# A two-layer graph block: layer 0 and the output projection as seven half-size products, factors of q, k, v fetched per step, last norm moved off VectorE

## The chip, the cores and the metric

The kernel runs on one core of one Trainium2 chip. The time is the device time of one execution in microseconds (us); each kernel was run several times, and medians are quoted. The "span" of a profile is about 1.8 us shorter than the run that it was taken from, because it begins and ends at instructions.

Engine names in the profile: PE is TensorE's matmuls, PEld its weight loads, DVE is VectorE, ACT is ScalarE, POOL is GpSimd, SP is the engine whose queue issues the transfers ("the sync queue").

## The reference, cut to what matters

All values are float32: 128 batches of 128 nodes with 512 features, two layers, each added to its own input.

```python
# layer 0: mix over neighbours, then a 512 x 512 weight
h = maximum(layernorm(x), 0)
x = x + (einsum('nm,bmd->bnd', adj, h) @ weight + bias)
# layer 1: attention over the graph's edges, 8 heads of 64
h = maximum(layernorm(x), 0)
q, k, v = split(h @ w_qkv)                 # w_qkv is 512 x 1536
attn = softmax(where(adj == 0, -inf, q @ k.T * 64**-0.5))
o = (attn @ v) @ w_proj + b_proj           # w_proj is 512 x 512
x = x + o + layernorm(o) * ln_gamma + ln_beta
```

## The kernel before

Each batch passes through a long chain: norm, mix with the adjacency, layer 0, norm, an exchange through DRAM that turns rows into columns, q, k, v, scores, softmax, a second exchange, attention, projection, last norm. A plan with a time for each piece (one batch per "slot") fixes the program order on every engine, so that TensorE always has the work of some batch to do while the others wait.

q, k and v are made for a group of four batches by seven products of half-size blocks instead of eight (a Strassen form): sums of blocks of the left operand are made by GpSimd, the sums of the weights once at the start, and the results are put together by additions that read PSUM. Layer 0 and the projection are whole products of 512 columns:

```python
def product(g, kind, k, p):                 # one of the seven, for q, k, v
    left = LEFT[g][k]
    for half in range(2):
        for c in range(2):
            ...                             # lhsT or rhs from wqk_sb / wv_sb, resident in SBUF
            nc.tensor.matmul(p[:, half, :], lhsT=lhsT, rhs=rhs, ...)      # 256 columns

def layer0(i, t):
    p = mm_psum("pl0")
    for c in range(C):                      # C = 4 blocks of 128
        nc.tensor.matmul(p, lhsT=YT[i][:, c, :], rhs=w0_sb[:, c, :], start=(c == 0), stop=(c == C - 1))
    put(t + 3.7, norm1, i, t + 3.7, p)

def project(i, t):
    ...                                     # the same with OT[i] and wp_sb
    put(t + 3.7, finish, i, t + 3.7, p)

def finish(i, t, p):
    o = work.tile([P, D], F32, name="o")
    nc.vector.tensor_tensor(o, p, bp_b, op=ALU.add)
    mean, rs = stats_of(o)
    t_ = work.tile([P, D], F32, name="t", bufs=2)
    nc.vector.scalar_tensor_tensor(t_, o, mean, gamma_b, op0=ALU.subtract, op1=ALU.mult)
    nc.gpsimd.tensor_tensor(o, o, X1.pop(i), op=ALU.add)
    put(t + 8, finish_out, i, t_, rs, o)    # second scalar_tensor_tensor, then the store
...
SLOT = 19.0
for i in range(-LOAD, B + 3):
    t = i * SLOT
    at(t + 0.5, scores, i)
    at(t + 3, project, i - 2)
    at(t + 11, layer0, i + 8)
    at(t + 15.8, attend, i - 1)
    ...                                     # put(time, function, ...) sorts all pieces by time
```

## Time and profile before

| | before |
|---|---|
| time, median of 3 | 2561.32 us |
| span of the profile | 2558.2 us |
| busy: TensorE, VectorE, GpSimd, ScalarE | 98, 66, 45, 38% |
| matmul instructions | 12545 |
| work in TensorE's stream (see below) | 2475.3 us |
| lost while filling, in mid-run, while draining | 47.9, 0.0, 35.1 us |

The lines of the profile that carry this are shown in the prediction. Between two matmuls of the same shape that follow each other without a wait, the trace gives a start-to-start time: 429 ns for 512 columns, 216 for 256, 112 for 128. Add these over the whole program order, with the measured 1.09 us of a batch's scores and 1.03 of its attention and about 0.1 us for each switch into and out of these two (they use part of the array; the first of them starts 0.31 us after its full-size predecessor instead of 0.22, and after them the second full-size one 0.32 us after the first), and you have the time of the stream if TensorE never had to wait: its **work**. At any point of the program, the time in the trace less the work up to there is what has been **lost** so far, be it to waits or to a slow clock. Filling is what is lost before the scores of batch 8, mid-run from there to the scores of batch 124, draining the rest.

The seven-product form puts its weights' sums in SBUF beside the weights, and the transfers took less than half of the DMA engines' time. This line of the profile's page of before gives the queue's packets, its MB, and the share of the time of 16 engines:

```profile
q1 hardware_dynamic: 262288, 342.54, 41.3%
```

### The profile page before, as it was taken

The numbers are of one execution on the slowest core, as the hardware profiler recorded it, in microseconds if no ns is written. First come the engines' busy times: TensorE is split into PE (matmuls) and PEld (weight loads), VectorE is DVE, ScalarE is ACT, GpSimd is POOL, SyncE is SP. The second block draws the span as 40 slices with busy tenths as digits, with TensorE's granted clock in tenths as the row PEclk, the third lists the DMA queues.
The fourth block names the chain that finished last, engine by engine and source line by source line (L and its number), as shares of the span: only waits on it lengthen the run. The fifth ranks groups of instructions, "written<-read, shape, count | busy, mean of one in ns | idle before, by whom it ended". The sixth has DMA issues, their size and how long they took to land.

```text
span 2558.2 us, 36517 instructions
## 1 busy us (share of the span) xinstructions
PE 2497.8 (98%) x12545; PEld 1749.4 (68%) x12545; DVE 1676.1 (66%) x3119; ACT 962.3 (38%) x2946; POOL 1153.4 (45%) x1030
## 2 busy tenths in 40 slices
PE   5999999999999999999999999999999999999996
PEld 3677776766767767777677676676767667767673
DVE  4466666666666667666666666666666666666665
ACT  2243343343334343334334334333333433433331
POOL 3444444444445435444444444444544444444332
PEclk8999999999999999999999999999999999999997
DMA  5244444444443443444444444444344344444333
GB/s 187 93 137 141 145 127 132 148 133 132 144 137 124 145 144 124 139 143 130 137 145 131 132 141 139 132 141 140 124 136 148 128 135 146 132 132 137 123 100 106
DMA packets 262472, 344.86 MB, mean 135 GB/s; under 512 B 28944, under 2 KB 161168, under 8 KB 262288
## 3 DMA queue, kind: packets, MB, share of 16 engines
q1 hardware_dynamic: 262288, 342.54, 41.3%
q8 instruction: 99, 1.62, 0.3%
q14 instruction: 85, 0.70, 0.1%
HBM read 174.65 MB, written 167.77 MB: 134 GB/s over the span
## 4 chain that ended last, share of the span: by engine, by line
PE 94%; issue 2%; POOL 1%; DVE 1%; DMA 0%; SPq 0%; ACT 0%; POOLq 0%; DVEq 0%; ACTq 0%
PE cx L239 26%; PE pl L183 17%; PE pp L331 17%; PE cy L239 13%; PE cz L239 7%; PE ps L278 5%; PE po L322 5%; PE pmix L174 4%; POOL rs L143 0%; POOL e L307 0%; DMA h1x<-d 0%; POOL o L341 0%; SPq L155 0%; DVE st L137 0%; ACT h L161 0%
## 5 line engine op out<-in xcount | busy, mean ns | idle before, releaser
L143 POOL TENSOR_TENSOR rs<-ve,minus_half 128x1 f32<-128x1 f32 x384 | 261.7, 681 | 726.7 <-DVE ve L141 725.6
L183 PE MATMUL pl<-w_sb,yT 128*128 128x512 f32 x1024 | 465.5, 598 | 4.3 <-DVE x L189 4.3
L331 PE MATMUL pp<-wp_sb,oT 128*128 128x512 f32 x1024 | 466.9, 599 | 1.4 <-ACT oT L404 1.4
L298 ACT ACTIVATE e<-s,mx 128x128 f32<-128x128 f32 x1024 | 394.1, 386 | 29.2 <-DVE mx L289 24.7
L169 POOL TENSOR_TENSOR x<-x,b_b 128x512 f32<-128x512 f32 x128 | 162.3, 1268 | 465.9 <-ACT h L161 463.4
L161 ACT ACTIVATE h<-x,shift,rs 128x512 f32<-128x512 f32 x256 | 208.3, 814 | 416.0 <-DVE shift L160 400.5
L183 PEld LDWEIGHTS pl<-w_sb,yT 128*128 128x128 f32 x1024 | 196.2, 192 | 198.0 <-issue 186.8
L331 PEld LDWEIGHTS pp<-wp_sb,oT 128*128 128x128 f32 x1024 | 196.5, 192 | 196.1 <-issue 187.5
L286 DVE TENSOR_TENSOR s<-ps,maskb 128x512 f32<-128x512 f32 x256 | 164.5, 684 | 171.1 <-PE ps L278 171.1
L337 DVE TENSOR_TENSOR o<-pp,bp_b 128x512 f32<-128x512 f32 x128 | 88.5, 692 | 273.0 <-PE pp L331 273.0
L198 POOL TENSOR_TENSOR x<-x,beta_b 128x512 f32<-128x512 f32 x128 | 162.4, 1269 | 196.1 <-ACT h L161 196.1
L239 PE MATMUL cy<-sum,wqk_sb 128*128 128x256 f32 x1024 | 246.7, 384 | 3.9 <-POOL sum L221 3.9
L239 PE MATMUL cx<-sum,wqk_sb 128*128 128x256 f32 x1024 | 248.5, 385 | 1.8 <-ACT qkT L404 1.8
L404 ACT COPY qkT<-cx 128x512 f32<-128x512 f32 x192 | 111.8, 582 | 360.4 <-PE cx L239 360.4
L307 POOL TENSOR_TENSOR e<-e,sm 128x1024 f32<-128x1024 f32 x128 | 244.5, 1910 | 4.1 <-DVE sm L306 4.1
L239 PE MATMUL cx<-h1T,wqk_sb 128*128 128x256 f32 x1024 | 245.0, 382 | 0.0
L239 PEld LDWEIGHTS cy<-sum,wqk_sb 128*128 128x128 f32 x1024 | 193.0, 191 | 72.5 <-issue 44.0
L404 ACT COPY oT<-po 128x512 f32<-128x512 f32 x128 | 75.1, 587 | 438.9 <-PE po L322 438.9
L345 DVE SCALAR_TENSOR_TENSOR t<-t,rs,o 128x512 f32<-128x512 f32 x128 | 226.5, 1770 | 4.3 <-POOL o L341 4.3
L239 PEld LDWEIGHTS cx<-h1T,wqk_sb 128*128 128x128 f32 x1024 | 189.6, 190 | 54.0 <-issue 29.9
L239 PEld LDWEIGHTS cx<-sum,wqk_sb 128*128 128x128 f32 x1024 | 187.1, 190 | 47.4 <-issue 22.1
L298 ACT ACTIVATION_READ_ACCUMULATOR e<-s,mx 128x1 f32 x1024 | 191.1, 187 | 0.0
(68 smaller groups left out, 3596.3 us busy)
## 6 DMA issues: line engine op xcount, KB each, us to landing
d<-e SPq DMA_DIRECT2D x128, 512.0 KB, 2.6
sx<-d SPq DMA_DIRECT2D x512, 128.0 KB, 2.9
x<-in_x_dram SPq DMA_DIRECT2D x130, 256.0 KB, 2.9
d<-h SPq DMA_DIRECT2D x128, 256.0 KB, 2.3
x1d<-x SPq DMA_DIRECT2D x128, 256.0 KB, 2.0
h1x<-d SPq DMA_DIRECT2D x512, 64.0 KB, 2.4
x1b<-x1d SPq DMA_DIRECT2D x128, 256.0 KB, 2.8
out_dram<-t SPq DMA_DIRECT2D x128, 256.0 KB, 3.0
```

The costliest lines, as they stand in the source:

```text
L143: nc.gpsimd.tensor_tensor(rs, ve, minus_half, op=ALU.pow)
L161: nc.scalar.activation(dst, src, AF.Relu, bias=shift, scale=rs)
L169: put(t + 5, lambda: nc.gpsimd.tensor_tensor(x_, x_, b0_b, op=ALU.add))
L183: nc.tensor.matmul(p, lhsT=YT[i][:, c, :], rhs=w0_sb[:, c, :], start=(c == 0), stop=(c == C - 1))
L198: nc.gpsimd.tensor_tensor(X1[i], X1[i], beta_b, op=ALU.add)
L239: nc.tensor.matmul(p[:, half, :], lhsT=lhsT, rhs=rhs, start=first and half == 0 and c == 0, stop=k in (3, 5, 6) and c == 1, skip_group_che ...
L286: nc.vector.tensor_tensor(s[:, e * C:(e + 1) * C, :], ps[e], m4, op=ALU.add)
L298: nc.scalar.activation(e[:, :, h, :], s[:, h, :].rearrange("p (q r) -> p q r", q=Q), AF.Exp, bias=shift[:, h:h + 1], scale=scale, accum_ou ...
L307: nc.gpsimd.tensor_tensor(e, e, sm.unsqueeze(1).unsqueeze(3).to_broadcast([P, Q, H, R]), op=ALU.mult)
L331: nc.tensor.matmul(p, lhsT=OT[i][:, c, :], rhs=wp_sb[:, c, :], start=(c == 0), stop=(c == C - 1))
L345: nc.vector.scalar_tensor_tensor(t_, t_, rs, o, op0=ALU.mult, op1=ALU.add)
L404: f(*a)
```

## The change

Layer 0 and the projection now also go by seven half-size products, on pairs of batches. That needs room: seven blocks of factors for each of the two weights are resident, and in exchange the factors of q, k, v are no longer. Their four sums are made at the start and written to DRAM, and each of the 21 steps of a group fetches its own factor (256 KB), four steps ahead. The last norm leaves VectorE, which has the new additions to do: ScalarE normalizes, GpSimd multiplies by gamma and adds. The schedule is remade, with a compressed beginning (`FILL`) and an end of its own for the last four batches.

The core of the diff, cut (`...`):

```diff
-    wqk_sb = const.tile([P, 7, 2, D], F32)
-    wv_sb = const.tile([P, 7, 2, D // 2], F32)
-    wp_sb = const.tile([P, C, D], F32)
+    w0_sb = const.tile([P, 7, 2, F], F32)          # F = 256
+    wp_sb = const.tile([P, 7, 2, F], F32)
...
+    def fetch(g, kind, k):
+        t = WQ[g, kind, k] = work.tile([P, 2, F], F32, name="wq", bufs=5)
+        plain = {0: (0, 0), 3: (1, 1), 5: (1, 0)}
+        nc.sync.dma_start(out=t, in_=qkv_block(kind, *plain[k]) if k in plain else SUMS[kind, k])
...
+    def pair_left(j, t, src, left, name):          # four sums on GpSimd, 256 columns each
+        y = src.pop(j)
+        left[j] = left_factors(t, 1.7, y[:, 0:2, 0, :], y[:, 2:4, 0, :], y[:, 0:2, 1, :], y[:, 2:4, 1, :], name)
+
+    def pair_chain(left, w_sb, tiles, addend):
+        def product(k, p, first, last):
+            for c in range(2):
+                nc.tensor.matmul(p[:, 0, :], lhsT=left[k][:, c, :], rhs=w_sb[:, k, c, :], ...)
+        ...                                        # results by additions of 256 columns on VectorE
+        return seven({"x": "d0", "y": "d1", "z": "z"}, product, start, results, 1.0)
...
-        t_ = work.tile([P, D], F32, name="t", bufs=2)
-        nc.vector.scalar_tensor_tensor(t_, o, mean, gamma_b, op0=ALU.subtract, op1=ALU.mult)
-        nc.gpsimd.tensor_tensor(o, o, X1.pop(i), op=ALU.add)
-    def finish_out(i, t_, rs, o):
-        nc.vector.scalar_tensor_tensor(t_, t_, rs, o, op0=ALU.mult, op1=ALU.add)
+        put(t + 1, lambda: nc.gpsimd.tensor_tensor(x1, x1, o, op=ALU.add))
+    def finish_out(i, t, mean, rs, x1):
+        n = work.tile([P, D], F32, name="t", bufs=2)
+        norm(AF.Identity, n, O.pop(i), mean, rs)
+        put(t + 1.5, lambda: nc.gpsimd.tensor_tensor(n, n, gamma_b, op=ALU.mult))
+        put(t + 4, finish_last, i, n, x1)          # gpsimd: n + x1, then the store
...
-    SLOT = 19.0
+    SLOT, FILL = 18.2, 7.0
+    def scores_at(i):
+        return when(i, 0) if i < LAST else when(LAST, -0.05) + (i - LAST) * 8.5
...
+    for n, (t, *a) in enumerate(steps):
+        put(steps[n - 4][0] + 0.1 if n >= 4 else t - 10, fetch, *a)
+    for kind, t in enumerate((when(-9, 0.2), when(-4, 0.0), when(-2, 0.1))):
+        put(t, combine_qkv, t + 7, kind)
```

## The prediction

> **What bounds the kernel now.** I read the page first: the busy shares, the chain that ended last, and the costliest groups.
>
> ```profile
> span 2558.2 us, 36517 instructions
> PE 2497.8 (98%) x12545; PEld 1749.4 (68%) x12545; DVE 1676.1 (66%) x3119; ACT 962.3 (38%) x2946; POOL 1153.4 (45%) x1030
> PE 94%; issue 2%; POOL 1%; DVE 1%; DMA 0%; SPq 0%; ACT 0%; POOLq 0%; DVEq 0%; ACTq 0%
> L183 PE MATMUL pl<-w_sb,yT 128*128 128x512 f32 x1024 | 465.5, 598 | 4.3 <-DVE x L189 4.3
> L331 PE MATMUL pp<-wp_sb,oT 128*128 128x512 f32 x1024 | 466.9, 599 | 1.4 <-ACT oT L404 1.4
> L239 PE MATMUL cx<-sum,wqk_sb 128*128 128x256 f32 x1024 | 248.5, 385 | 1.8 <-ACT qkT L404 1.8
> ```
>
> TensorE fills the span and nearly the whole chain; VectorE, the next, is at 66%. So the time is what TensorE's stream costs plus the times it has no work. Layer 0 (L183) and project (L331) are the only whole products left; q, k, v (L239) already go by seven half-size products. Each fp32 matmul of the program is two instructions (1024 for 4 x 128).
>
> A group's mean (598 ns) is one instruction's latency, not its cost. The timeline of TensorE in mid-run gives the cost, from start to start:
>
> ```profile
> 1204.82 1.16 PE L278 MATMUL ps<-qkT 64*128 64x128 f32 x16
> 1205.91 1.99 PE L239 MATMUL cx<-h1T,wqk_sb 128*128 128x256 f32 x8
> 1207.74 3.60 PE L331 MATMUL pp<-wp_sb,oT 128*128 128x512 f32 x8
> 1211.17 1.89 PE L239 MATMUL cy<-sum,wqk_sb 128*128 128x256 f32 x8
> 1212.90 1.05 PE L174 MATMUL pmix<-adjT,h 128*128 128x128 f32 x8
> 1213.79 1.89 PE L239 MATMUL cx<-sum,wqk_sb 128*128 128x256 f32 x8
> 1215.52 3.60 PE L183 MATMUL pl<-w_sb,yT 128*128 128x512 f32 x8
> 1218.95 1.89 PE L239 MATMUL cy<-sum,wqk_sb 128*128 128x256 f32 x8
> ```
>
> No idle stands between them. A whole product takes 3.43 us (1211.17 - 1207.74; 429 ns per instruction of 512 columns), a q, k, v step 1.73 us (216 ns per 256), a mix 0.89. From pp to the next pp (1226.64) it is 18.90 us with five steps; a group of four batches has 21, so 0.25 x 1.73 more: 19.33 us per batch, x 128 = 2474 us.
>
> The rest, 2558 - 2474 = 84 us, is filling and draining. Windows show where:
>
> ```profile
> 0.00:60.00 60.00, 30.20 (x84) 17.08 (x85) 26.30 (x63) 11.54 (x17) 17.49 (x25) 0.87 0.55 189
> 60.00:120.00 60.00, 54.30 (x230) 40.18 (x229) 23.72 (x57) 19.16 (x42) 24.58 (x25) 0.96 0.27 88
> 2500.00:2530.00 30.00, 18.19 (x87) 10.67 (x87) 22.10 (x33) 10.73 (x50) 10.29 (x8) 0.82 0.35 117
> 2530.00:2558.00 28.00, 15.09 (x48) 6.89 (x47) 9.80 (x14) 1.17 (x2) 6.41 (x6) 0.68 0.22 75
> ```
>
> The columns after the window are its length, then PE, PEld, DVE, ACT, POOL busy with counts, granted clock, DMA share, GB/s. In the windows between 120 and 2500 us that I asked for, TensorE is 100% busy. I put some 42 us of loss in the first 75 us (until the last gap at 74.8) and some 37 us after the scores of batch 124 (2480.8), the rest in rounding and the lower clock.
>
> **What the Trainium skill says.** "Perfetto Trace Analysis", Identifying the Most-Contended Engine: matmul busy share is no measure of how near TensorE is to its limit. Agreed here: busy hides that the stream could hold less work. "TensorE: Matmul & The Clock Gate", Step-by-step: back to back, a matmul costs its columns and its drain overlaps the next one's. The trace agrees: 216 and 429 ns for 256 and 512 columns, so two halves cost no more than a whole. Weight loads (192 ns each) fit under 216 ns. "SBUF — State Buffer", Who interferes with whom: a VectorE instruction with two SBUF inputs contends with a GpSimd instruction that reads SBUF; with at most one, and no 2-port mode, it doesn't. The trace agrees: the last SCALAR_TENSOR_TENSOR (L345) varies from 858 to 2382 ns where its like (L340) is even, while additions with one PSUM input stay near 690.
>
> ```profile
> L345 DVE SCALAR_TENSOR_TENSOR t<-t,rs,o 128x512 f32<-128x512 f32 x128 | 226.5, 1770 | 4.3 <-POOL o L341 4.3
> L340 DVE SCALAR_TENSOR_TENSOR t<-o,mv,gamma_b 128x512 f32<-128x512 f32 x128 | 94.9, 742 | 0.0
> ```
>
> "GPSIMD Engine Reference", Elementwise — side-by-side cycle accounting: a two-input add of 2048 fp32 takes 4497 ns, 2.2 ns per element; here 512 take 1270, so about 0.15 us is fixed and 256 should take an estimated 0.71.
>
> **The change, part by part.**
>
> TensorE. Per pair of batches and layer, eight 512-column matmuls (2 x 3.43 = 6.86 us) become seven products of two 256-column matmuls: 7 x 4 x 0.216 = 6.05 us. Saved: 0.81 us per pair and layer; over 64 pairs and two layers 104 us. The rest of the stream is the same in kind and number. New stream: 2474 - 104 = 2370 us, 18.5 us per batch. All of this is on the path, since TensorE is never idle in mid-run.
>
> VectorE, beside it. Leaves: both SCALAR_TENSOR_TENSOR (226.5 + 94.9) and two additions of 512 columns (88.3 + 88.5), 498 us. Comes: 2 x 64 x 7 = 896 additions of 256 columns; the weight sums at the start took 1216 ns for 1024 columns and 678 for 512, so 256 columns are worth 0.27 us, and 690 ns for 512 gives an estimated 0.42 for 256, 380 us in all, and 128 shifts of 0.21, 27 us. 1676 - 498 + 407 = 1585 us, 65% of the new time. None of the new additions has two SBUF inputs, so none can be held by GpSimd.
>
> ScalarE: 128 Identity of 0.81 us, 104 us: 1066.
>
> GpSimd: two more 512-column operations per batch (256 x 1.27 = 325 us) and 512 sums of 256 columns for the left factors (512 x 0.71 = 364): 1153 + 689 + 5 for the projection weights = 1847 us, 75%. It becomes the second engine.
>
> DMA: 672 fetches of 256 KB, 176 MB. In the trace a packet of 1 KB takes 46 ns (median) and one of 2 KB 84; 288 fetches of 256 x 1 KB and 384 of 128 x 2 KB make 7.5 ms of packet time, over 16 queues 470 us. With today's 41.3% of 2558 (1056 us), 1526 us, 62%; some 212 GB/s. A fetch is issued four steps (13.9 us) ahead; a load of its size landed in 2.9 us.
>
> Filling. The first step of q, k, v starts at 62.9 us and stalls until 74.8, waiting for sums and copies. The changed order loads layer 0's weights first, puts off the others, and needs only two pairs of layer 0 before the first group. From before's row times (first mix at 14.3, some 10 us per pair at the low clock, 10 us for norm and exchange) I estimate a full stream from 57 us, with less done by then (6 mixes, 3 pairs, 23.5 us). Loss 33 us plus 5 for hitches: 38 instead of 42.
>
> Draining. Before, from the scores of batch 124 to the end are 77 us. After, the last four scores follow one another as fast as one exponent tile allows: exponentials 4.6, divide 1.9, write out 2.6, with semaphores 10 us each; scores of 127 thus near 29 us; then 20 us to attend, and copy, GpSimd sums, seven products, statistics, last norm on two more engines and the store, some 20. That is 69 us, with 35 us of work in it: 34 lost.
>
> Sum: 2370 + 38 + 34 = 2442, plus 3 us (2561.3 run against 2558.2 span), plus 7 us, a guess, for small stalls in mid-run: 2452 us.
>
> **The rivals.**
>
> 1. Halves cost more than the columns say. Read by busy time (466 / 1024 = 455 ns, 248.5 / 1024 = 243 ns), a pair saves 7.28 - 6.80 = 0.48 us, 61 us in all, giving 2495. Against: the start-to-start times above, in a stream of the same 256-column shape.
>
> 2. GpSimd sets the pace. At 75% and in strict order, with a divide that waits for the exponentials, it may run late. I laid its order of two slots (36.4 us) out by hand: the divide can start about 10 us into a slot; then its queue is at most some 6 us behind, while the left sums of project have 7 to 8 us and those of layer 0 over 10. So no stall of TensorE; if I am wrong by a microsecond per batch, +128 us: 2580.
>
> 3. Weights arrive late or the sync queue is blocked: it issues in order, about 0.43 us each, 19.25 per batch instead of 14 (8.3 of 18.5 us), and waits for the divide stand in it. 10 us of slack stands against it. If half of the steps waited 0.5 us: 672 x 0.25 = 168 us more, 2620.
>
> 4. PSUM: layer 0 and project now share two single banks, the attention products two. Product 2 can't start before product 0 has been read; between them lie 0.245 of a slot, 4.5 us, of which the matmuls take 0.9 and the addition with its waits about 1; VectorE's wait before the reciprocal comes after that read. Expected: a few us at most in all.
>
> **Range and chances.** The 104 us are firm. Filling and draining may be off by 15 us either way; small stalls add from 0 to 40. That gives 2428 to 2490. 2% faster is 2510, which takes 58 us of stalls beyond my sum: rivals 2 to 4 in earnest, 7 in 100. Slower by over 2% needs over 160 us of them, 1 in 100.
>
> **What would show it.** Right: whole mid-run windows with TensorE at 100%; starts 0.86 us apart for each half-size product of two matmuls; 18.5 us per batch; GpSimd near 75%, DMA near 62%, VectorE near 65%; even durations on VectorE. Wrong: TensorE rows released by the weight tile (late fetch), by the left sums (GpSimd), or by an addition on VectorE (banks), each repeating per slot; or starts farther apart than 216 ns per 256 columns.

## The result, and the profile after

The changed kernel takes **2469.68 us** (median of 4, 2468.1 to 2471.64) against 2561.38 of the kernel before (median of 4, 2560.69 to 2562.83). The ratio is 0.964 (95% interval 0.9625 to 0.9658). Ratios here and below are the mean time of one kernel's runs over that of the other's of the same rounds, so not quite the ratio of the medians that are quoted. It is 92 us faster: inside the predicted range, 18 us above the predicted 2452. All outputs are right.

The page of after, from the top: the span, the busy line, the DMA queue, the chain that ended last.

```profile
span 2467.9 us, 42898 instructions
...
PE 2401.2 (97%) x14081; PEld 2044.7 (83%) x14081; DVE 1560.7 (63%) x3639; ACT 1034.6 (42%) x3074; POOL 1759.0 (71%) x1802
...
q1 hardware_dynamic: 399856, 521.89, 68.9%
...
PE 92%; POOL 1%; DVE 1%; ACT 0%; issue 0%; DMA 0%; POOLq 0%; DVEq 0%; ACTq 0%
```

TensorE still carries the chain, now 92% of it instead of 94. It has 12% more instructions and 97 us less busy time. GpSimd has become the second engine, as expected, and the queue's share went from 41.3 to 68.9%.

The timeline of TensorE in mid-run of after (start, length, engine, line, tiles, shapes, number of instructions):

```profile
1216.11 1.16 PE L339 MATMUL ps<-qkT 64*128 64x128 f32 x16
1217.20 1.99 PE L322 MATMUL pc<-wq,hsum 128*128 128x256 f32 x8
1219.03 1.03 PE L261 MATMUL pd<-w_sb,yT 128*128 128x256 f32 x4
1219.89 1.89 PE L322 MATMUL pc<-wq,hsum 128*128 128x256 f32 x8
```

One half-size product of layer 0 (the row with `w_sb,yT`) takes 0.86 us (1219.89 - 1219.03), so seven of them take 6.05 us for two batches where two whole ones took 6.86. There is no bracket with a wait behind any row. That is so from the scores of batch 8 to those of batch 116, over which a batch takes 18.512 us; before it was 19.336.

Windows of after (length, then busy us with counts of PE, PEld, DVE, ACT, POOL, granted clock, DMA share, GB/s):

```profile
0.00:60.00 60.00, 34.75 (x137) 27.53 (x137) 29.17 (x81) 14.16 (x20) 30.12 (x41) 0.91 0.69 219
60.00:120.00 60.00, 53.59 (x249) 45.33 (x250) 32.40 (x73) 17.49 (x39) 32.17 (x33) 0.91 0.66 213
...
1200.00:1260.00 60.00, 60.00 (x353) 51.48 (x352) 40.23 (x94) 25.43 (x79) 42.04 (x43) 1.00 0.72 221
...
2430.00:2468.00 38.00, 18.60 (x80) 12.92 (x80) 11.98 (x30) 4.31 (x6) 24.81 (x26) 0.72 0.29 97
```

Mid-run is full at full clock. The two ends are not: TensorE is busy for less than half of the last 38 us, and the clock stays at 0.91 until 120 us, where before it was at 0.96 in the second window. The account of all this, with the predicted terms:

| us | before | predicted | after | after less predicted |
|---|---|---|---|---|
| work in the stream | 2475.3 | 2370 | 2369.1 | -0.9 |
| lost before the scores of batch 8 (filling) | 47.9 | 38 | 53.5 | +15.5 |
| lost from there to the scores of batch 124 | 0.0 | 7 | 2.7 | -4.3 |
| lost after (draining) | 35.1 | 34 | 42.6 | +8.6 |
| from span to run | 1.9 | 3 | 1.8 | -1.2 |
| sum | 2560.1 | 2452 | 2469.7 | +17.7 |

The sums are those of the runs that were profiled (2560.06 and 2469.65 us). The predicted 3 us is the median of before, 2561.3, less the span of another of its runs.

So the change removed 106.2 us of work, and gave back 5.6 us of it in filling, 2.7 at the end of mid-run, and 7.5 in draining.

**Where the filling is lost.** Before the first q, k, v step there are 24.6 us of work in after (seven mixes and three pairs of layer 0); the step starts at 64.2 us, so 39.6 us are lost before it and 13.9 after it. The first rows below are from TensorE's timeline of after, where a bracket gives the wait before a row and what ended it; the next is from VectorE's timeline; the last three from the sync queue's.

```profile
62.34 2.07 PE L261 MATMUL pd<-w_sb,yT 128*128 128x256 f32 x4 [5.44 <-DVE x L233]
64.21 3.62 PE L322 MATMUL pc<-h1T,wq 128*128 128x256 f32 x8
```

```profile
60.19 1.46 DVE L294 STREAM_TRANSPOSE h1T<-h1x 128x512 f32<-128x512 f32 x2 [5.41 <-DMA h1x<-d]
```

```profile
50.92 1.05 SPq L130 DMA_DIRECT2D sx<-in_L_gnn_w_qkv_dram  x2
52.01 1.00 SPq L130 DMA_DIRECT2D pT<-in_L_gnn_w_qkv_dram  x2
...
53.58 5.62 SPq L196 DMA_DIRECT2D h1x<-d  x8
```

Read from below: the exchange that turns batches of the first group (`h1x<-d`) stands in the sync queue behind four blocks of weights, the second kind of q, k, v, whose sums are not needed for many steps. VectorE waits 5.4 us for the exchange before it can transpose. Behind the transposition, in VectorE's program order, stand the additions of a layer 0 product (L233), and TensorE waits 5.4 us for those. After a wait the clock is low too: those four matmuls take 2.07 us, in mid-run 1.03. The Trainium skill ("TensorE: Matmul & The Clock Gate", Part 1: The HAM clock gate) says that an idle TensorE falls to half its clock and needs some 3.4 us of activity to get it back; the trace agrees, with a factor of two in exactly those rows. The 13.9 us after the first step are 6.7 us in five waits, and for most of the rest that clock: a mean of 0.90 over the 36 us from 64 to 100 and 0.97 over the next 50 is an estimated 5 us.

**Where the draining is lost.** Scores of 124 to scores of 127, from there to the attention of 127, to the last matmul, to the end:

| us | before | predicted | after |
|---|---|---|---|
| scores of 124 to scores of 127 | 39.3 | near 29 | 30.0 |
| to the attention of 127 | 21.7 | 20 | 28.5 |
| to the last matmul, to the end | 8.0 + 8.5 | some 20 | 11.3 + 12.5 |
| sum | 77.4 | 69 | 82.3 |

The last four batches follow each other as planned. Then two stretches, to the attention of 127 and to the end, are longer than predicted and longer than in before. The end of GpSimd's timeline of after shows the second of them:

```profile
2458.80 1.26 POOL L403 TENSOR_TENSOR x1b<-x1b,o 128x512 f32<-128x512 f32 x1
2460.02 2.48 POOL L409 TENSOR_TENSOR t<-t,gamma_b 128x512 f32<-128x512 f32 x2
2462.46 2.48 POOL L413 TENSOR_TENSOR t<-t,x1b 128x512 f32<-128x512 f32 x2
```

The two batches of the last pair end together, and their last norms run in turn on one engine: three operations of 1.26 us for each. In before one batch stood alone at the end, and after its statistics GpSimd had one such operation to do and VectorE two instructions of 0.75 us.

### The profile page after: what moved, and what is told of

The parts are those of the page before. It is cut to its first block, busy times and chain, and to the rows that moved or that the text cites. A ratio compares the mean times of both kernels' runs of the same rounds, so it can differ in the third digit from the quotient of the medians.

```text
span 2467.9 us, 42898 instructions
## 1 busy us (share of the span) xinstructions
PE 2401.2 (97%) x14081; PEld 2044.7 (83%) x14081; DVE 1560.7 (63%) x3639; ACT 1034.6 (42%) x3074; POOL 1759.0 (71%) x1802
## 3 DMA queue, kind: packets, MB, share of 16 engines
q1 hardware_dynamic: 399856, 521.89, 68.9%
## 4 chain that ended last, share of the span: by engine, by line
PE 92%; POOL 1%; DVE 1%; ACT 0%; issue 0%; DMA 0%; POOLq 0%; DVEq 0%; ACTq 0%
PE pc L322 39%; PE pd L261 26%; PE pz L322 7%; PE ps L339 6%; PE pz L261 5%; PE po L383 5%; PE pmix L247 4%; POOL t L409 0%; ACT e L359 0%; POOL x1b L403 0%; POOL e L368 0%; DVE s L347 0%; DVE mx L349 0%; POOL t L413 0%; POOL osum L205 0%
## 5 line engine op out<-in xcount | busy, mean ns | idle before, releaser
L322 PE MATMUL pc<-hsum,wq 128*128 128x256 f32 x2048 | 489.2, 382 | 1.1 <-ACT qkT L326 0.6
L322 PEld LDWEIGHTS pc<-hsum,wq 128*128 128x128 f32 x2048 | 387.3, 191 | 58.4 <-ACT qkT L326 1.2
L359 ACT ACTIVATE e<-s,mx 128x128 f32<-128x128 f32 x1024 | 397.1, 391 | 16.7 <-DVE mx L350 12.5
L261 PE MATMUL pd<-wp_sb,osum 128*128 128x256 f32 x1024 | 265.3, 383 | 5.5 <-POOL osum L205 5.3
L261 PE MATMUL pd<-w_sb,ysum 128*128 128x256 f32 x1024 | 265.3, 383 | 3.5 <-POOL ysum L205 3.5
L322 PE MATMUL pc<-wq,hsum 128*128 128x256 f32 x1024 | 245.4, 383 | 2.6 <-ACT v L326 2.6
L322 PE MATMUL pc<-h1T,wq 128*128 128x256 f32 x1024 | 246.7, 384 | 0.0
L322 PEld LDWEIGHTS pc<-wq,hsum 128*128 128x128 f32 x1024 | 191.5, 190 | 32.8 <-ACT v L326 4.2
L261 PEld LDWEIGHTS pd<-wp_sb,osum 128*128 128x128 f32 x1024 | 191.0, 192 | 32.3 <-POOL osum L205 8.5
L322 PEld LDWEIGHTS pc<-h1T,wq 128*128 128x128 f32 x1024 | 193.2, 191 | 29.1
L261 PEld LDWEIGHTS pd<-w_sb,ysum 128*128 128x128 f32 x1024 | 190.9, 192 | 29.3 <-POOL ysum L205 5.5
```

Source lines behind the costliest of these rows:

```text
L261: nc.tensor.matmul(p[:, 0, :], lhsT=left[k][:, c, :], rhs=w_sb[:, k, c, :], start=first and c == 0, stop=last and c == 1, skip_group_check ...
L322: nc.tensor.matmul(p[:, half, :], lhsT=lhsT, rhs=rhs, start=first and half == 0 and c == 0, stop=last and c == 1, skip_group_check=True)
L359: nc.scalar.activation(e[:, :, h, :], s[:, h, :].rearrange("p (q r) -> p q r", q=Q), AF.Exp, bias=shift[:, h:h + 1], scale=scale, accum_ou ...
```

## The experiments

Twelve kernels ran, all variants of the changed one, in three groups on three chips, each group with its own runs of the kernel before (2560.72, 2561.28 and 2560.83 us). The changed kernel itself was not run again in these groups; its own group had 2561.38 us for before, so the four groups agree within 0.7 us. Letters in the quoted expectations name theories: A is the one that I held, the others are its rivals in that run.

### The gain itself: e1 and e2

The projection alone goes back to whole products.

```diff
-        return pair_chain(LEFT2.pop(j), wp_sb, (O[2 * j], O[2 * j + 1]), (bp_b, bp_b))    # seven half-size products
...
+                for c in range(C):              # cols is slice(0, D): 4 matmuls of 512 columns per batch
+                    nc.tensor.matmul(p[:, cols], lhsT=y[:, c, n, :], rhs=wp_sb[:, c, cols], ...)
```

> The changed kernel with project alone put back to whole products (four matmuls of 512 columns per batch, no left sums for it). Theory A (a matmul costs its columns and nothing else): the period of a batch in mid-run goes from 18.51 to 18.92 us (+0.41), the stream gains 52 us, the drain gives back some 3 to 8 us, so about 2515 to 2520 us against 2470. Rival B (halves carry a fixed cost per instruction, as the busy times suggest): the project halves had won only about 30 us, so about 2495.

Measured: 2510.86 us, ratio 0.981 (0.979 to 0.9822), so 41 us slower than after. The time per batch is 18.924 us, 0.412 more; half of 0.81 us is 0.405. The rival of a fixed cost beside the columns falls here. The time is some 4 us below theory A's range, because the ends gave back more than expected: the filling loses 50.2 us and the drain 33.7, where after loses 53.5 and 42.6. The drain is taken up below.

The second kernel computes the same with each whole product cut into two halves of 256 columns, so twice the instructions for the same columns.

```diff
+            for half in range(2):
+                cols = slice(half * F, (half + 1) * F) if True else slice(0, D)
+                for c in range(C):
+                    nc.tensor.matmul(p[:, cols], lhsT=y[:, c, n, :], rhs=wp_sb[:, c, cols], ...)
```

> As e1_project_whole, but each whole product of 512 columns is cut into two of 256 columns: the same columns in twice the instructions. Theory A (columns only): the same as e1_project_whole within 3 us, period 18.92 us. Rival B (fixed cost per instruction, 243 against 228 ns per 256 columns by busy time): 2048 x 243 - 1024 x 455 ns = 32 us more than e1_project_whole, period 19.17.

Measured: 2512.65 us, ratio 0.981 (0.9796 to 0.9825); 18.944 us per batch, 0.02 more than e1. The projection's rows in TensorE's timelines, first of e1, then of e2:

```profile
1220.71 3.60 PE L400 MATMUL pp<-wp_sb,oT 128*128 128x512 f32 x8
1224.14 1.89 PE L322 MATMUL pc<-hsum,wq 128*128 128x256 f32 x8
```

```profile
1221.94 3.62 PE L400 MATMUL pp<-wp_sb,oT 128*128 128x256 f32 x16
1225.40 1.89 PE L322 MATMUL pc<-hsum,wq 128*128 128x256 f32 x8
```

From the product to the next row 3.43 us with 8 instructions and 3.46 with 16: the columns cost, and cutting them into twice the instructions adds next to nothing. So the seven-product form gains what it saves in columns, one part in eight.

### Was the move of the norm needed: e3

The last norm goes back to VectorE for all batches (shown in effect: the old lines stay in the file, and an early return skips them).

```diff
-        norm(AF.Identity, n, O.pop(i), mean, rs)
-        put(t + 1.5, lambda: nc.gpsimd.tensor_tensor(n, n, gamma_b, op=ALU.mult))
-        nc.gpsimd.tensor_tensor(n, n, x1, op=ALU.add)
+        nc.vector.scalar_tensor_tensor(n, o, mean, gamma_b, op0=ALU.subtract, op1=ALU.mult)
+        nc.vector.scalar_tensor_tensor(n, n, rs, x1, op0=ALU.mult, op1=ALU.add)
```

> The changed kernel with the last norm alone put back on VectorE (two SCALAR_TENSOR_TENSOR per batch). Theory A (TensorE bounds mid-run, the move of the norm bought nothing there): the period stays at 18.51 us; the drain is 3 to 8 us shorter because two GpSimd operations and a ScalarE one leave the last chain; 2462 to 2468 us. Rival C (VectorE with two SBUF inputs is held up by a GpSimd that is busy over 60% of the time, and evacuations come late): the last SCALAR_TENSOR_TENSOR goes over 2 us in the mean, the period rises by 0.2 us or more, 2495 or more.

Measured: 2464.40 us, ratio 0.9625 (0.9611 to 0.9639), some 5 us *faster* than after (the two intervals overlap, but the traces show the place: the last two stretches of the drain are 9.5 and 9.5 us, 4.8 less than in after); 18.512 us per batch, as after; VectorE busy 69%, GpSimd 61%. Its two groups, from the view of groups by line (busy us and mean ns, then the idle before them):

```profile
L420 DVE SCALAR_TENSOR_TENSOR t<-t,rs,x1b 128x512 f32<-128x512 f32 x128 | 97.5, 762 | 80.8 <-POOL x1b L406 80.8
L405 DVE SCALAR_TENSOR_TENSOR t<-o,mv,gamma_b 128x512 f32<-128x512 f32 x128 | 95.9, 749 | 0.0
```

The first of these is the instruction that took 1770 ns in the kernel before. It has the same two SBUF inputs, and GpSimd is busier than it was then (61% against 45), and it takes 762 ns. The order differs: VectorE is now idle before it for 80.8 us in total, until a sum of GpSimd's is done, so that it starts when that engine has just finished an operation. The two traces bear this out. In before, 126 of its 128 executions overlapped GpSimd's divide of the exponentials and took 1786 ns in the mean (up to 2386), the other two 751; in e3, 124 overlapped nothing of GpSimd's and took 749. What counted was which instruction meets which, not how busy the other engine is. So in mid-run the move of the norm bought nothing up to batch 116 and some 3 us from there to 124 (see the table of accounts), and at the end it cost; rival C, that VectorE would be held up without the move, falls.

### How much room the transfers have: e4, e5, e12

Each factor is fetched a second time into a tile that nothing reads.

```diff
+        t2 = work.tile([P, 2, F], F32, name="wq2", bufs=2)
+        nc.sync.dma_start(out=t2, in_=qkv_block(kind, *plain[k]) if k in plain else SUMS[kind, k])
```

> The changed kernel with every q, k, v weight fetched a second time into a tile that nobody reads: 176 MB more. Theory A (fetches are hidden with about 10 us of slack): DMA share goes from 69% to 90% or more, the period stays under 18.7 us, filling costs up to 10 us more: 2470 to 2490 us. Rival D (transfers stand close to being the bound, landing times grow past the four steps of lead): the period goes over 19 us, 2530 or more.

Measured: 2575.77 us, ratio 1.0064 (1.0027 to 1.0102): the whole gain is gone. 19.302 us per batch. A mid-run window of it, then what TensorE waited for between 120 and 2400 us (us in total, times, longest):

```profile
1200.00:1260.00 60.00, 59.30 (x349) 50.19 (x346) 37.59 (x91) 25.41 (x74) 48.88 (x51) 1.00 0.89 278
```

```profile
PE pd L263 <- DVE x L235: 39.5, 45, 2.0
PE pc L324 <- DMA wq<-wt: 20.7, 24, 2.2
```

At a share of 0.89 the factors arrive late at times, and everything else on the queue too: in the same stretch GpSimd waits 409 us in total for the reload of a residual (`x1b`), its queue runs late, and so do VectorE's additions. Factors now took 4.1 and 5.0 us to land (medians), 3.4 and 3.9 in after. Rival D, the transfers, is thus real at twice the fetches and absent at once. The kernel doubles two things, the bytes and the issues in the sync queue, and does not tell them apart.

The next two kernels issue the fetches later: two steps ahead, and three.

```diff
-        put(steps[n - 4][0] + 0.1 if n >= 4 else t - 10, fetch, *a)
+        put(steps[n - 2][0] + 0.1 if n >= 4 else t - 10, fetch, *a)     # e5; n - 3 in e12
```

> The changed kernel with each q, k, v weight fetched two steps ahead instead of four (about 7 us instead of 14; a fetch lands in 3.4 to 3.9 us). Theory A (10 us of slack in the fetch): the period stays under 18.6 us and the time within 8 us of the changed kernel's 2470. Rival D (waits in the sync queue's order use up most of the lead): TensorE waits for the weight tile, the period rises by 0.3 us or more, 2510 or more.

Measured: 2550.20 us, ratio 0.9952 (0.9938 to 0.9965), 80 us slower than after, 19.093 us per batch. Theory A, that 10 us of slack stand behind a lead of four steps, fell. What TensorE waited for in e5 between 120 and 2400 us:

```profile
PE pc L322 <- DMA wq<-wt: 32.3, 46, 2.1
PE pz L322 <- DMA wq<-in_L_gnn_w_qkv_dram: 14.5, 9, 2.2
```

With another 3.9 us for the same tile in the other bank, the waits for factors are 51 us in that window; the clock was at half for 10.2 us between the scores of 8 and 124, an estimated 5 us more. The rest of the 78.6 us that e5 lost there is not placed. The sync queue's own waits in that window, the two largest (the output's store, and the store of an exchange):

```profile
SPq L414 <- POOL t L413: 439.7, 116, 6.7
SPq L191 <- ACT h L185: 330.0, 60, 6.9
```

A fetch that is issued behind such a store is issued late.

> The changed kernel with each q, k, v weight fetched three steps ahead (about 10.5 us). Two steps cost 81 us, four none. If the sync queue's order eats some 3 to 6 us of the lead and a fetch lands in 3.8 us, three steps nearly suffice: period 18.5 to 18.6 us, 2470 to 2482 us. If it eats more than that in part of the steps, the period is 18.7 us or more and the time over 2490.

Measured: 2472.13 us, ratio 0.9656 (0.9642 to 0.9669), 18.512 us per batch; in the same window TensorE waited three times, 2.9 us in all, for a factor. A step takes 3.53 us (18.512 / 5.25), so leads of 14.1, 10.6 and 7.1 us give 2470, 2472 and 2550 us. A factor lands 3.4 to 3.9 us after it is issued, so the rest of the needed lead is spent in the queue, behind stores that wait for their results, as e5's rows show. The slack of the changed kernel is between 3.5 us and 7, not 10.

### The drain: e6, e7, e10

For the last six batches alone the norm goes to VectorE, as in e3.

```diff
+        if i >= 122:
+            ...
+            nc.vector.scalar_tensor_tensor(n, o, mean, gamma_b, op0=ALU.subtract, op1=ALU.mult)
+            nc.gpsimd.tensor_tensor(x1, x1, o, op=ALU.add)
+            put(t + 2.5, finish_vector, i, n, rs, x1)      # the second one, and the store
```

> The changed kernel with the last norm on VectorE for batches 122 to 127 alone, halves and all else as they are. Theory A (of the 8 us that draining lost, the norm through ScalarE and GpSimd makes about half): time without work after the scores of batch 116 goes from 44.7 to about 40 us, 2464 to 2467 us; mid-run unchanged at 18.51 us. Rival E (the pair structure, waiting for the partner and the left sums, makes nearly all of it): within 2 us of 2470.

Measured: 2463.03 us, ratio 0.9621 (0.9608 to 0.9635), 6.7 us faster than after. Its stretches are 27.0, 28.1, 9.5 and 9.4 us where after has 30.0, 28.5, 11.3 and 12.5. The last two, 4.9 us together, are the norm's. The first, 3 us, is not: in both traces TensorE waits 3.2 us after the same matmul, and in after the next product then takes 2.07 us, in e6 1.13. That is the clock, and e9 below, with the same order, has 30.1 there. The norm thus makes 4.9 us at the very end, about half of the 8 us, as theory A had it; the time is 1 us below A's range, with the clock's help. Rival E's "nearly all" falls, but the pair structure has a part of its own, in the 28 us: e1 and e2 differ from after in the projection alone, and there this stretch is 21.7 and 21.4 us, as in before, and the drain loses 33.7 and 32.1 us in all.

The next kernel also makes the last three pairs' projections whole, to spare the wait for a pair and its sums.

```diff
+        if j >= 61:
+            for n in (a, b):
+                t = max(attend_at(n) + 2.5, when(LAST, 0.75))
+                put(t, project_whole, n, t)     # 256-column halves from the blocks kept, and one fetched again
+                put(t - 4, reload, n)
+                ...
```

> As e6_tail_norm, and project of batches 122 to 127 by whole products (eight matmuls of 256 columns per batch, from the blocks kept and one block fetched again), each batch as soon as it is attended. Theory A: 2.4 us more stream, but no waiting for the partner or for the left sums on GpSimd: the time without work after batch 116 goes to 34 to 37 us, 2458 to 2463 us. Rival F (the softmax of the last batches alone sets the drain): no better than e6_tail_norm, 2464 to 2468.

Measured: 2474.68 us, ratio 0.9662 (0.9649 to 0.9675), 12 us slower than e6. The last part is shorter, 8.1 and 8.2 us, but the scores of 127 come 39.1 us after those of 124 instead of 27.0: in my order they stand behind the attention of batch 124 and its whole product, and that attention waits 5.2 us for its probabilities. The try was at fault, so another was made with the scores first and only two pairs:

```diff
-                t = max(attend_at(n) + 2.5, when(LAST, 0.75))
+                t = max(attend_at(n) + 2.5, scores_at(B - 1) + 1.1)     # and j >= 62
```

> e6_tail_norm with project of batches 124 to 127 by whole products, but now behind the scores of batch 127 in TensorE's order. Theory A (e7_tail_both lost because its whole products stood in front of the scores of 126 and 127 and so held up the softmax that sets the drain): scores of 127 start within 50 us of the end again, 2460 to 2465 us. Rival H (whole products cost time in the drain by themselves, long blocks at a low clock): 2470 or more.

Measured: 2470.18 us, ratio 0.9646 (0.9633 to 0.9659): theory A as stated fell. The end is as short as in e7 (8.1 and 8.2 us), and the scores of 127 come after 29.7 us, but their attention takes 36.7 us more. The sync queue of e10:

```profile
2425.17 0.34 SPq L411 DMA_DIRECT2D x1b<-x1d  x1
2425.56 0.43 SPq L191 DMA_DIRECT2D d<-e  x1
```

The reload of a residual, put earlier with the projection that it serves, waits for a free buffer until 2425.2, and the store of the exponentials of batch 126 (`d<-e`) stands behind it; in e6 that store went out at 2414.1. There is one tile of exponentials, so those of 127 could start only at 2429.5 (2417.7 in e6). Both tries thus carried a fault of their own in an order, and whether whole products for the last batches alone help the drain **stays open**; used for all batches they do, in e1 and e2. What the two tries do show is that the last 24 us of after can be 16.

### The filling, and all together: e8, e9, e11

In e8 the weights of the second kind of q, k, v are loaded later, their sums and those of the third kind are made later, the blocks of the projection are loaded later, and the first pair's transpositions wait until their exchange has surely landed.

```diff
-        put(when(i + 2, 0.57), flip, a)
+        late = (-5, 0.32) if j == 0 else None
+        put(when(*late) if late else when(i + 2, 0.57), flip, a)
...
-    for kind, t in enumerate((when(-9, 0.2), when(-4, 0.0), when(-2, 0.1))):
-        put(t, combine_qkv, t + 7, kind)
-    put(when(-6, 0.5), load_square, wp_sb, w_proj)
+    for kind, t in enumerate((when(-9, 0.2), when(-3, 0.02), when(-2, 0.1))):
+        put(t, combine_qkv, t + (7, 11, 13)[kind], kind)
+    put(when(-1, 0.0), load_square, wp_sb, w_proj)
```

> The changed kernel with the start alone reordered: the transposes of the first pair stand behind the second pair's additions on VectorE, the blocks for k's and v's sums and the projection weights are loaded later, and the sums stand later on VectorE. Theory A (filling loses 53 us because VectorE stands in order before data that have not landed, with the additions that free TensorE's banks behind it): the time without work before batch 8 goes from 53.5 to 44 to 50 us, 2461 to 2466 us. Rival G (the path of the first group through norm, exchange and sums is what takes the time, whatever stands around it): within 2 us of 2470.

Measured: 2460.42 us, ratio 0.9605 (0.9592 to 0.9618), 9.3 us faster than after; the filling loses 46.4 us instead of 53.5, at the same 18.512 us per batch. Theory A, the order of the sync queue and of VectorE, holds; the edits were made together, and which of them counts most is not told apart. The rows of TensorE's timeline of e8 that answer to those of after:

```profile
56.24 1.13 PE L261 MATMUL pd<-w_sb,yT 128*128 128x256 f32 x4 [2.89 <-DVE x L233]
57.21 3.14 PE L322 MATMUL pc<-h1T,wq 128*128 128x256 f32 x8
```

The wait for the additions is 2.9 us instead of 5.4, another of 3.5 us for the same additions is gone, and the first q, k, v step starts at 57.2 us, seven earlier. The loss after it is unchanged (13.8 us, 13.9 in after).

> e8_fill and e6_tail_norm together. If the two ends are independent, their gains add: 9 us at the start and 7 at the end off 2470, so 2453 to 2456 us, faster than both kernels; without work 46 us before batch 8 and 37 after batch 116. If something common sets them (a bound elsewhere), one gain vanishes: 2460 to 2464.

e9 is e8 and e6 in one. Measured: **2453.69 us**, ratio 0.9582 (0.9569 to 0.9595), 16.0 us faster than after: the two repairs add (9.3 and 6.7; the runs of one kernel spread over 3 to 6 us, so the exact sum is chance). This version beats both kernels, and is the one to keep.

> e8_fill with e10_tail_whole: the sum of their gains; 2450 to 2456 us if theory A holds for e10_tail_whole, over 2458 if rival H holds.

e11 is e8 and e10 in one. Measured: 2460.32 us, ratio 0.9609 (0.9595 to 0.9622), 9.9 us faster than e10 and 6.6 slower than e9; its stretches in the drain are those of e10 (29.8, 36.8, 8.1, 8.2 us), with the same cause. Rival H's number held.

The accounts of all twelve in one place (us; each from one trace, and the filling of kernels with the same beginning differs by up to 4 us from trace to trace: 42.4 to 46.4 for e8, e9 and e11):

| kernel | work | per batch | lost filling | lost 8 to 124 | lost draining | span |
|---|---|---|---|---|---|---|
| after | 2369.1 | 18.512 | 53.5 | 2.7 | 42.6 | 2467.9 |
| e1 project whole | 2421.0 | 18.924 | 50.2 | 2.9 | 33.7 | 2507.7 |
| e2 the same, cut | 2423.1 | 18.944 | 50.3 | 3.3 | 32.1 | 2508.8 |
| e3 norm on VectorE | 2369.1 | 18.512 | 53.4 | 5.8 | 34.7 | 2463.0 |
| e4 fetch twice | 2369.1 | 19.302 | 60.4 | 98.8 | 45.8 | 2574.1 |
| e5 two steps ahead | 2369.1 | 19.093 | 61.1 | 78.6 | 41.5 | 2550.2 |
| e6 norm in the tail | 2369.1 | 18.512 | 52.4 | 2.7 | 34.3 | 2458.5 |
| e7 whole in the tail | 2371.7 | 18.512 | 54.1 | 2.7 | 45.1 | 2473.6 |
| e8 filling | 2369.1 | 18.512 | 46.4 | 2.7 | 42.8 | 2461.1 |
| e9 = e8 + e6 | 2369.1 | 18.512 | 42.4 | 2.7 | 36.5 | 2450.7 |
| e10 whole, scores first | 2370.8 | 18.512 | 54.8 | 2.7 | 41.2 | 2469.6 |
| e11 = e8 + e10 | 2370.8 | 18.512 | 44.3 | 2.8 | 41.4 | 2459.3 |
| e12 three steps ahead | 2369.1 | 18.512 | 51.4 | 8.0 | 42.3 | 2470.8 |

## Why the prediction was right or wrong

**TensorE's stream: right to 1 us.** The predicted 0.81 us per pair and layer is what e1 took away for one layer (0.412 us per batch), and e2 shows that it is by columns alone. 18.5 us per batch was 18.512. The first rival (a fixed cost per half, 2495 us) is excluded by e2.

**No stalls in mid-run: right, and the 7 us were a little too many.** 0.6 us were lost between the scores of batches 8 and 116, 2.7 until those of 124. The hand-laid order of GpSimd held: in mid-run TensorE never waited for a sum of left factors, and no addition came too late for a bank. Rivals 2 and 4 did not happen.

**The engines beside it: right in kind.** VectorE 1561 us (1585 predicted), ScalarE 1035 (1066), GpSimd 1759 (1847). The new additions of VectorE took 422 ns (0.42 estimated):

```profile
L267 DVE TENSOR_TENSOR x<-pd,x 128x256 f32<-128x256 f32 x256 | 107.9, 422 | 106.0 <-PE pd L261 98.1
```

The 256-column sums of GpSimd took 0.73 us (0.71). GpSimd has less than predicted partly because its power instruction (`rs`), which the prediction left at before's mean of 681 ns, now takes 549 (384 x 0.13 = 51 us); in before some of them took over 900.

**The DMA share: the size was off, 68.9% for 62.** The step that failed is "a packet of 1 KB takes 46 ns (median) and one of 2 KB 84". Those medians are unchanged in after, but a share is a sum, and sums go by means: 57 and 99 ns, which make 566 us of the predicted 470 (288 x 256 x 57 + 384 x 128 x 99 ns, over 16). The remaining 3 points are the old packets, which became longer as well (those of 4 KB from 162 to 185 ns). The fetches landed somewhat later than the 2.9 us that the prediction took:

```profile
wq<-wt SPq DMA_DIRECT2D x384, 256.0 KB, 3.4
wq<-in_L_gnn_w_qkv_dram SPq DMA_DIRECT2D x288, 256.0 KB, 3.9
```

**The third rival: rightly put at a few chances, on a wrong reason.** "10 us of slack" was the lead less the landing time. e5 and e12 show that the sync queue uses up to between 3 and 7 us of the lead itself, waiting for results before stores. The lead of four steps was enough by 3.5 to 7 us.

**Filling: the term of the sum that was most mis-sized, 38 us against 53.5.** Three steps of it failed. First, "I estimate a full stream from 57 us" took only durations, not the order of the sync queue and of VectorE; the first step came at 64.2, and e8, which changes just these orders, starts it at 57.2. That is 6.1 us (39.6 lost before the step, 33.5 by the prediction's own figures). Second, "plus 5 for hitches" was 13.9, and e8 did not change it: waits of 6.7 us, and for the most part a low clock after each, which the prediction did not count. Third, it stands against a wrong base: before's own filling loses 47.9, not 42. The prediction had seen the 5 us left over ("in rounding and the lower clock") and did not carry them into the sum for after.

**Draining: the next, 34 against 42.6.** The last four scores took 30.0 us ("near 29"). The step that failed is what follows. "Some 20" to the end was 23.8: the last norm of the pair's two batches runs in turn on GpSimd, and e6 takes back 4.9 us. "20 us to attend" was 28.5 (28.1 in e6 and e9), and what that step left out is the projection by halves beside it: in e1 and e2, where the projection alone is whole again, it is 21.7 and 21.4. In after the divide of batch 127 starts 14.5 us after its scores (ready at 2426.6 us, started at 2430.05, behind a left sum and norm operations on GpSimd), and the transposition of its probabilities 12.7 us after that, behind additions and statistics of the projection on VectorE. In e1 these are 10.0 and 10.4 us; in e6, without the norm on GpSimd, 13.2 and 13.6. Which of the left sums, the additions and their places in the orders makes the 7 us is not shown. The work left after the scores of 124 was also 39.7 us, not 35; this is in the stream's sum and doesn't count twice.

The range held because the firm term was firm, and in part by luck. The two ends together erred by 24.1 us, more than the 15 that they had been given; the time stayed inside because most of the 40 us allowed for stalls in mid-run was not used (2.7). The range is also not quite what its parts say: 2445 without stalls, plus 15 and 40, is 2500, not 2490.

## What to carry to other kernels

When one engine's stream is full, add up its program order with start-to-start times: the work comes out to 1 us, and everything else in the time can be looked for where it is lost. In a pipeline that is full in mid-run, what a change adds to the shared in-order queues is paid at the two ends, so give filling and draining orders of their own, and remember that after a wait of some microseconds TensorE also runs slow for a while (at half clock for 3.4 to 10.2 us at a time in the trace of after). Moving work to an engine with time to spare is not free if nothing was waiting: here it bought next to nothing in mid-run and cost about 5 us at the end.

## What the Trainium skill lacked or had wrong

- "TensorE: Matmul & The Clock Gate" times a matmul by its columns, but has no time for a float32 one. Here it is two instructions of 429 ns each for 512 columns, 858 ns in all.
- "TensorEngine Tiling (Array Packing)" says that going over to matmuls that use part of the array drains TensorE, but not what it costs. Here the first matmul of the scores or the attention starts 0.31 us after a full-size one instead of 0.22, and after them the second full-size one starts 0.32 us after the first.
- "DMA: Bandwidth & Descriptors" gives bandwidth and a fixed cost of a transfer, but nothing from which to choose the lead of a fetch in a queue that also stores results. Here leads of 14.1, 10.6 and 7.1 us gave 2470, 2472 and 2550 us, with 3.4 to 3.9 us from issue to landing; and a DMA share of 69% left TensorE without a wait between the scores of batches 8 and 116, where one of 89% (278 GB/s, with twice the issues) came with 0.79 us more per batch.
- "SBUF — State Buffer" is right that the order of issue decides who is held up, but has no durations for this pair. Here the same VectorE instruction took 1786 ns in the mean where it overlapped GpSimd's divide and 750 where it overlapped nothing.
